# Adjacency masks by casting transfers, x in five loads, powers in pairs, and a search that alone holds the adjacency rooms

## The chip, the cores and the metric

The kernel runs on one core of a Trainium2 chip. Its engines are TensorE (PE; its weight loads, PEld, overlap its matmuls), VectorE (DVE), ScalarE (ACT), GpSimd (POOL) and SyncE (SP, which only issues transfers). ACT and POOL can issue transfers too. Each engine works through its own instructions in order and waits for the others by semaphores. The metric is the time of one execution on the device in microseconds (us), as a median over runs.

## The reference, cut to what matters

x has 2708 rows of 256, adj is 2708 x 2708, float32, about 1.2% of it nonzero, with values up to 1e9. Two layers, each a graph layer and a transformer or expert layer:

```python
# layer 0, graph: adj is added to the logits, so each row's largest entry wins the softmax
x = x + softmax(leaky(f1 + f2.T) + adj) @ h + bias          # h = layernorm(x) @ weight
# layer 0, attention and experts: causal, rotary positions, 4 query and 2 key heads of 64
u = layernorm(x)
z = u + attention(rmsnorm(u)) @ wo.T
x = x + z + top2_of_8_experts(rmsnorm(z))
# layer 1, graph: the mask is adj != 0, or the diagonal
x = x + sigmoid(softmax(where((adj != 0) | eye, leaky(a_src + a_dst.T), -inf)) @ Xp)   # Xp = layernorm(x) @ W.T + b
x = x + top2_of_8_experts(layernorm(x))
```

Because entries of adj are so large, the kernel replaces the first softmax by a lookup: for each row it finds the index of the largest entry and adds that row of h. Flags test whether this holds, and a general network runs if not.

## The kernel before, in words

Rows are cut into NT = 22 tiles of 128 (the last has 20). There are four stages: `first` (0 to about 505 us of the profile), `experts_blocks` of layer 0 (to about 808), `second` (to about 1148), `experts_blocks` of layer 1.

**The planner.** In `first` and `second` every piece of work is a step given to `Plan.add`: an engine, a length in us, a function that emits the instructions, the steps it needs, buffers it takes and gives back, a rank, and `lands`, the time a transfer still takes after its issue. `Plan.issue` simulates the engines with these figures and always emits, among the steps that can start soonest, the one of lowest rank. The figures are used for the order only: what an engine really waits for are semaphores on the data. Before a PE step that the plan sees start late, `fill` emits throwaway matmuls into a free PSUM bank (tile `nobody`), so many that 75% of the gap is filled at 0.24 us each, in gaps of at least 1 us.

**The first stage.** `project` (two tiles at a time, rank -1) takes the statistics of x on DVE (L268, L270, L918), a power -1/2 per tile on POOL (L922), transposes x on PE (L929), multiplies by the centred weight (L949), scales on ACT (L956) and stores the result to the table `hd` in memory (L961). POOL adds the bias row into x (L933). x arrives in three loads of 4, 17 and 1 tiles (L856, L859).

`tile_in` runs once per tile t, with rank t. SP loads 128 rows of adj into one of three rooms in `arena` (L990) together with the rotary table `tb` (L992). DVE finds the eight largest entries (`top`, L995) and the index (`index`, L999). ACT narrows the same room to bfloat16 in two halves (`narrow`, L1009; POOL clears the padding, L1006 and L1008), and SP saves the halves to the matrix `mb` in memory (L1012). A room has two names in the plan, `adj` and `low`: `index` gives back the one and the second narrowing the other, and the next load into it takes both. POOL fetches the chosen rows of `hd` and adds them into x by an indirect transfer (L1017); this needs all stores to `hd`. Then come statistics (DVE), powers (POOL), the q/k/v product (PE), rotary positions on POOL (`both`: L804 to L806 and L1064), transposes, and copies into qT and kT.

`pair` does attention for two tiles of queries, with rank t0 + 2.5: scores on PE (L1121), exponentials on ACT (L1127), the causal mask on POOL (L1136), values on PE (L1147), sums of exponentials on DVE (L1161, L1166; for the first tiles on PE), reciprocal (L1204), the output product, and additions into x. After groups of tiles, `route` chooses two experts per token and POOL scatters the rows to the experts' lists `xs` (`send`, L1830). At the end `early_blocks` runs three expert blocks whose tokens are already complete, after the last scores. The next stage begins with loads of expert rows from `xs`.

**The second stage** reads `mb` by transposing transfers on SP (L1570, L1566), the first of them at 809.8 us, turns it into 0 and 1 on DVE, and sums neighbours on PE (L1603). It has a plan of its own.

Transfers that POOL issues share one queue (q0), those of SP another (q1), those of ACT a third (q10); all run on the same 16 DMA engines. In the cut below, functions that the change touches are shown.

Of the kernel before, what the change touches and what calls it, by code (L numbers as in the profile page):

```python
# [10 lines left out]
F32 = mybir.dt.float32  # L11
# [9 lines left out]
P = 128  # L21
# [53 lines left out]
class Plan:  # L75
# [8 lines left out]
    UNIT = 0.24  # L84
    FILL = 0.75
    GAP_MIN = 1.0
# [64 lines left out]
def adj_ffn_kernel(ctx, tc, x, adj, vecs, bias_rows, tab, w_gnn0, w_gnn1, wqkv, wo,  # L151
# [41 lines left out]

    ident = const.tile([P, P], F32, name="ident")
# [33 lines left out]
    allones = const.tile([P, P], F32, name="allones")  # L228
    nc.gpsimd.memset(allones, 1.0)

# [138 lines left out]

    def route(add, tiles, ready, copied, cleared, layer, XB, xs, pool, turn_tile, turn_bank, gate_tile, gate_bank, rank):  # L370
# [127 lines left out]
        if layer == 0:  # L498
            a = [add("ACT", 0.6, lambda t=t: squares(t), [ready[t - t0]], rank=rank) for t in tiles]
            a = add("DVE", 0.3, mean, a, rank=rank)  # L500
            scaled = add("POOL", 0.9, power, [a], rank=rank)
        last = None
        for pair in pairs:
# [10 lines left out]
            if gate_tile is None:  # L514
                a = add("ACT", 0.25, lambda pair=pair: keep(pair), [a], give=[turn_bank], rank=rank)
            last = a
        a = add("DVE", 3.2, choose, [last], rank=rank)
        b = add("ACT", 0.5, exps, [a], rank=rank)
# [3 lines left out]
        return [add("POOL", 2.7, lambda t=t: send(t), [b, c] + cleared, rank=rank + 6, lands=2.0) for t in tiles]  # L522


    def some_blocks(add, layer, blocks, fetched, needs, weights, xs, acc, new, named, rank):

        joins = []
        for k, (e, j, before) in enumerate(blocks):
# [68 lines left out]
            a = add("ACT", 0.7, back, [a], take=[names["xT"]], give=[names["mm"]], rank=r)  # L597
# [3 lines left out]
            a = add("ACT", 1.4, gate, [a], take=[names["sl"], names["hT"]], rank=r)  # L601
            a = add("DVE", 1.4, times, [a], give=names["up"] + [names["sl"]], rank=r)
# [4 lines left out]
            joins.append(add("POOL", 1.6, join, [a], give=[names["ys"]], rank=r))  # L607
        return joins

    def early_blocks(add, layer, needs, sent, *rest):  # L610
        blocks = [(e, j, (needs if layer == 0 else []) + sum([sent[t] for t in sent if t < before_t], []))
                  for e, j, before_t in EARLY[layer]]

        return some_blocks(add, layer, blocks, [XR[:, k, :] for k in range(len(blocks))], needs, *rest)
# [194 lines left out]
    def first(X, XB, norms, tops, hd, mb, xs, acc, arena, load_weights):  # L809
# [11 lines left out]
        with ExitStack() as s:  # L821
# [24 lines left out]
            def tr_tile():  # L846
                return mm_tile().rearrange("p (k c) -> p k c", c=P)

            plan = Plan(mm=2, mv=4, ix=4, tb=6, st=2, o=1, zs=1, e=4, xg=3, hT=3,
                        z=2, qk=2, es=1, ob=2, yT=2, mb=2, rT=1, adj0=1, adj1=1, adj2=1, low0=1, low1=1, low2=1)  # L850
# [3 lines left out]
            loads = []  # L854
            for a, b in ((0, 4), (4, NT - 1)):
                loads.append(add("SP", 0.5, lambda a=a, b=b: nc.sync.dma_start(  # L856
                    out=X[:, a:b, :], in_=x[a * P:b * P, :].rearrange("(t p) c -> p t c", p=P)),
                    rank=-9.0, lands=1.5 + 0.4 * (b - a)))
            loads.append(add("SP", 0.5, lambda: nc.sync.dma_start(  # L859
                out=X[:rows(NT - 1), NT - 1, :], in_=x[(NT - 1) * P:N, :]), rank=-9.0, lands=9.0))  # L860
            rest = add("ACT", 2.0, load_rest, rank=-9.0, lands=8.0)
# [19 lines left out]
            a = add("SP", 1.2, load_wq, loads, take=["e"], rank=1.5, lands=3.0)  # L881
# [21 lines left out]
            wg_in = add("SP", 0.0, lambda: None, rank=-9.0, lands=3.0)  # L903
# [5 lines left out]
            def project(t0):  # L909
# [5 lines left out]
                def stats(t):  # L915
                    r = rows(t)
                    v["mv", t], v["pv", t] = moments(X[:r, t, :], r), small.tile([P, 1], F32, tag="pv", name="pv")
                    nc.vector.tensor_scalar(v["pv", t][:r], v["mv", t][:r, 1:2], 1.0, 1e-5, ALU.mult, ALU.add)  # L918

                def power(t):  # L920
                    r = rows(t)
                    nc.gpsimd.tensor_tensor(out=rsx[:r, t:t + 1], in0=v["pv", t][:r], in1=mhalf[:r, 0:1], op=ALU.pow)  # L922
# [43 lines left out]

                x_in = [loads[0]] if t0 < 4 else [loads[1]] if t0 + 2 < NT else loads[1:]
                s_ = {t: add("DVE", 0.85, lambda t=t: stats(t), x_in, take=["mv"], rank=rank) for t in two}
                c = [add("POOL", 0.6, lambda t=t: power(t), [s_[t]], give=["mv"], rank=rank) for t in two]
                a = add("PE", 0.5, turn, x_in, take=["mm"], rank=rank - 1.0)  # L970
                for t in two:
                    biased.append(add("POOL", 0.8, lambda t=t: bias(t), [a, s_[t], rest], rank=rank + 1.5 + t / NT))
                a = add("ACT", 0.6, back, [a], take=["yT"], give=["mm"], rank=rank - 1.0)
                a = add("PE", 1.75, times, [a, centred[0]], take=[bank], give=["yT"], rank=rank)
# [4 lines left out]
            made, loaded = {}, {}  # L979
            rsv = ap.tile([P, NT, 2], F32, name="rsv")  # L980
            nmv = ap.tile([P, NT], F32, name="nmv")

            def tile_in(t):
# [4 lines left out]
                def load():  # L988
                    v["a"] = arena[:, t % 3 * N:(t % 3 + 1) * N]
                    nc.sync.dma_start(out=v["a"][:r], in_=adj[t * P:t * P + r, :])  # L990
                    v["tb"] = adjp.tile([P, 2 * HD], F32, tag="tb", name="tb", bufs=6)
# [5 lines left out]
                def index():  # L997
                    v["ix"] = small.tile([P, 8], mybir.dt.uint32, tag="ix", name="ix")
# [1444 lines left out]
```

## Time and profile before

| | us |
|---|---|
| median of three runs (lowest, highest) | 1467.53 (1466.63, 1470.84) |
| the profiled execution | 1465.13 |
| its span from the first to the last instruction | 1463.3 |
| PE, PEld, DVE, ACT, POOL busy | 1385.9, 1006.3, 775.9, 555.3, 525.3 |
| q1, q0 moved | 162.32 MB, 25.71 MB |

Times in views of the trace are us from the span's start unless marked ns. A line of a group gives: line and engine, operation, output and inputs by name, shape, count; then busy time and mean ns of one; then the idle time of the engine just before these instructions and what ended it. A line of waits gives: who waited for what, us in total, times, longest. A line of a stretch gives: the stretch, its length, busy time of each engine with instruction counts, the granted PE clock as a share, the mean busy share of the DMA engines, GB/s. Fillers count as PE busy time.

### The profile page before, as it was taken

How to read it: one execution, taken by the hardware profiler on the slowest of the kernel's cores; microseconds unless marked ns; L12 is line 12 of the kernel's file. 1: busy time of each engine (PE TensorE's matmuls, PEld its weight loads, DVE VectorE, ACT ScalarE, POOL GpSimd, SP SyncE). 2: the span in 40 equal slices, each digit the busy share in tenths (PEclk: the TensorE clock that was granted, in tenths of full speed). 3: DMA queues.
4: the chain of work that ended last, by engine and by line, in shares of the span. 5: the costliest groups of instructions: out<-in, count | busy, mean ns of one | idle time of the engine just before them, and what ended most of it. 6: DMA issues, size and time to landing. Idle time of an engine off the chain costs nothing.

```text
span 1463.3 us, 20902 instructions
## 1 busy us (share of the span) xinstructions
PE 1385.9 (95%) x7218; PEld 1006.3 (69%) x7218; DVE 775.9 (53%) x1680; ACT 555.3 (38%) x1104; POOL 525.3 (36%) x677
## 2 busy tenths in 40 slices
PE   6988989989999999999999899999999999999996
PEld 5643433433343888888788878888768888878885
DVE  5688999985676432222222474768565322322221
ACT  2576867655545322222221444434432211111110
POOL 5576668874224312222222210022334222222222
PEclk9899999999999999999999999999999999999998
DMA  7588756540001277777512770616321687666211
GB/s 268 192 290 287 252 197 226 158 155 31 8 16 64 46 205 185 168 175 197 105 18 26 159 166 1 133 39 151 108 73 58 148 214 187 194 185 129 24 19 21
DMA packets 260056, 193.05 MB, mean 132 GB/s; under 512 B 168008, under 2 KB 232104, under 8 KB 257232
## 3 DMA queue, kind: packets, MB, share of 16 engines
q1 hardware_dynamic: 235638, 162.32, 38.0%
q0 software_dynamic: 20032, 25.71, 9.7%
q10 hardware_dynamic: 4270, 3.58, 0.8%
q8 instruction: 59, 0.97, 0.3%
q14 instruction: 57, 0.47, 0.1%
HBM read 119.81 MB, written 56.11 MB: 120 GB/s over the span
## 4 chain that ended last, share of the span: by engine, by line
PE 77%; DVE 8%; POOL 6%; DMA 5%; issue 2%; ACT 1%; SPq 0%; POOLq 0%; DVEq 0%; ACTq 0%
PE pup L2115 23%; PE po L1603 15%; PE y L2130 13%; PE o L1147 4%; PE stt L1121 4%; PE up L562 3%; DMA X<-hd,ix 3%; PE pup L2146 3%; PE y L2180 1%; DVE yT L1204 1%; DVE es L1166 1%; PE po L949 1%; DVE ix L999 1%; POOL ra L804 1%; DVE tops L995 1%
## 5 line engine op out<-in xcount | busy, mean ns | idle before, releaser
L2115 PE MATMUL pup<-xTs,arena 128*128 128x256 f32 (+2 forms) x1320 | 249.7, 348 | 0.6 <-ACT xTs L2098 0.6
L2115 PEld LDWEIGHTS pup<-xTs,arena 128*128 128x128 f32 (+1 forms) x1320 | 218.5, 189 | 27.2 <-PE y L2180 1.5
L1603 PE MATMUL po<-hb,PT 128*128 128x257 f32 (+2 forms) x968 | 227.6, 389 | 2.9 <-DVE PT L1596 2.9
L2119 ACT ACTIVATE sl<-pup 128x256 f32<-128x256 f32 (+1 forms) x210 | 73.5, 350 | 368.9 <-PE pup L2115 325.4
L1603 PEld LDWEIGHTS po<-hb,PT 128*128 128x128 f32 (+2 forms) x968 | 176.7, 189 | 42.8 <-issue 13.3
L2120 DVE TENSOR_TENSOR hT<-sl,pup 128x256 f32<-128x256 f32 (+1 forms) x210 | 79.6, 380 | 225.8 <-ACT sl L2119 220.5
L1127 ACT ACTIVATE e<-stt 128x1024 f32<-128x1024 f32 (+1 forms) x132 | 125.5, 986 | 93.5 <-PE stt L1121 63.8
L1166 DVE TENSOR_TENSOR es<-es,e 128x1024 f32<-128x1024 f32 x104 | 137.8, 1325 | 29.8 <-ACT e L1127 22.0
L622 POOL DMA_INDIRECT out<-ys,XR x44 | 68.0, 1545 | 234.2 <-DVE ys L2133 149.5
L622 POOL DMA_INDIRECT acc<-ys,XR x44 | 68.3, 1553 | 215.4 <-DVE ys L2133 120.8
L1121 PE MATMUL stt<-qT,kT 64*128 64x512 f32 (+1 forms) x528 | 133.4, 616 | 4.3 <-ACT e L1127 3.9
L2130 PE MATMUL y<-arena,hT 128*128 128x256 f32 x612 | 137.3, 380 | 0.0
L2130 PEld LDWEIGHTS y<-arena,hT 128*128 128x128 f32 x612 | 114.6, 190 | 19.7 <-DVE hid L2154 4.9
L1830 POOL DMA_INDIRECT xs<-XR,place x88 | 93.2, 1059 | 91.8 <-DVE mk L1590 40.2
L1147 PE MATMUL o<-e,V 128*64 128x512 f32 (+1 forms) x528 | 122.4, 586 | 0.0
L1581 ACT ACTIVATE E<-sb,dcol 128x768 f32<-128x768 f32 (+1 forms) x88 | 75.3, 859 | 108.4 <-DVE PT L1596 106.5
L2133 DVE TENSOR_SCALAR ys<-y,XR 128x256 f32<-128x256 f32 x71 | 34.4, 484 | 133.7 <-PE y L2130 133.7
L2115 PE MATMUL pup<-xTs,room 128*128 128x256 f32 (+3 forms) x528 | 99.9, 346 | 0.0
L1121 PEld LDWEIGHTS stt<-qT,kT 64*128 64x128 f32 x528 | 44.7, 188 | 76.5 <-issue 63.0
L2115 PEld LDWEIGHTS pup<-xTs,room 128*128 128x128 f32 (+1 forms) x528 | 85.4, 189 | 9.8 <-PE y L2180 0.8
L1147 PEld LDWEIGHTS o<-e,V 128*64 128x64 f32 x528 | 32.9, 136 | 68.5 <-issue 53.2
L995 DVE MAX8 tops<-arena 128x8 f32<-128x2708 f32 (+1 forms) x22 | 65.3, 2970 | 1.5 <-DMA arena<-in_adj 1.5
(319 smaller groups left out, 1972.1 us busy)
## 6 DMA issues: line engine op xcount, KB each, us to landing
more<-in_w SPq DMA_DIRECT2D x48, 640.0 KB
arena<-in_adj SPq DMA_DIRECT2D x21, 1354.0 KB
arena<-in_w SPq DMA_DIRECT2D x36, 640.0 KB
mb<-mb SPq DMA_DIRECT2D x44, 352.0 KB
xs<-none SPq DMA_DIRECT2D x16, 536.0 KB
room<-in_w SPq DMA_DIRECT2D x12, 640.0 KB
pieces<-xs SPq DMA_DIRECT2D x200, 32.0 KB
acc<-X SPq DMA_DIRECT2D x21, 128.0 KB
```

The source lines that it names most:

```text
L622: i = nc.gpsimd.indirect_dma_start(out=acc[:, :], out_offset=bass.IndirectOffsetOnAxis(ap=tokens.bitcast(I32), axis=0), in_=ys, in_offset= ...
L995: nc.vector.max(out=tops[:r, t, :], in_=v["a"][:r])
L1121: nc.tensor.matmul(st[:r, g, c0(sb):], kT[a:b, sb * P:sb * P + r], qT[a:b, t0 + (sb == t0 + 1):t0 + 2, :, :], start=True, stop=True)
L1127: nc.scalar.activation(e[:r, :, c0(sb):], v[sb, "st"][:r, :, c0(sb):], AF.Exp, scale=1.0 / HD ** 0.5)
L1147: nc.tensor.matmul(v["o"][g * HD:(g + 1) * HD, c:], V[:r, sb, g * HD:(g + 1) * HD], v[sb][:r, g, c:], start=(n + i == 0), stop=(n + i == t ...
L1166: nc.vector.tensor_tensor(es, es, v[sb][:r, :, c:], ALU.add)
L1581: nc.scalar.activation(e[:q, :n], sb[:q, i0:i1], AF.Exp, bias=dcol[:q, j:j + 1], scale=SLOPE - 1.0)
L1603: nc.tensor.matmul(v["po", i][:r, :F], v["PT", j][:q, a:a + r], hb[:q, j, :], start=(j == 0), stop=(j == NT - 1))
L1830: i = nc.gpsimd.indirect_dma_start(out=xs[:, :], out_offset=bass.IndirectOffsetOnAxis(ap=at, axis=0), in_=src, in_offset=None)
L2115: nc.tensor.matmul(pp[:to, i, :B, :], wn[:, c, :], xT[:, c, :B, :], start=(c == 0), stop=(c == KC - 1))
L2120: nc.vector.tensor_tensor(hT[:, n, :B, :], sl[:, :B, :], pp[:, 1, :B, :], ALU.mult)
L2130: nc.tensor.matmul(y, hT[:, n, b, :], w[3][:, n, :], start=(n == 0), stop=(n == NHC - 1))
```

## The change

- **Masks.** `narrow`, `save` and the padding memsets go, and with them the names `low`. After all tiles' steps there are 22 new POOL steps, `cast`: each is one transfer from adj in memory to `mb` in memory that turns float32 into bfloat16. They need the last adjacency load, are chained in the plan one after the other (1.2 us of POOL, 6 us to land), and have ranks from 22 to 32.5. Seven small transfers on SP (`blank`) write the padding of `mb`. The second stage still reads `mb` as before.
- **Search.** The load of a room has rank t - 2 and `tb` a step of its own; `top` and `index` have rank t and not t + 2; only `index` gives the room back. The indices stay in one tile `ixs` and no longer rotate.
- **Start.** x comes in loads of 2, 4, 8, 7 and 1 tiles. `allones` is set first on POOL, and fillers multiply it by itself, not by `before`. Statistics and powers of two tiles share a buffer and one power instruction.
- **Planner.** Many lengths and some `lands` are new; fillers fill 85% of a gap at 0.22 us each, from gaps of 0.7 us. Some needs are added that the order kept by chance so far: routing choices in sequence (`chosen`), additions of expert results after the stores of the same rows (`standing`), last products and joins after the earlier ones. Both stages end in two empty steps behind the scatters, which let `fill` act there. The weights' fold moves from rank 45 to rank 1, the q/k/v product to rank t - 2.5.

```diff
-    UNIT = 0.24
-    FILL = 0.75
-    GAP_MIN = 1.0
+    UNIT = 0.22
+    FILL = 0.85
+    GAP_MIN = 0.7
...
+    allones = const.tile([P, P], F32, name="allones")
+    nc.gpsimd.memset(allones, 1.0)
     ident = const.tile([P, P], F32, name="ident")
...
-            for a, b in ((0, 4), (4, NT - 1)):
-                loads.append(add("SP", 0.5, lambda a=a, b=b: nc.sync.dma_start(
+            loads, ends = [], (2, 6, 14, NT - 1)
+            for a, b in zip((0,) + ends, ends):
+                loads.append(add("SP", 0.55 * (b - a), lambda a=a, b=b: nc.sync.dma_start(
...
+                def power():
+                    for at, q in [((0, 2), P)] if rows(t0 + 1) == P else [((0, 1), P), ((1, 2), rows(t0 + 1))]:
+                        n = at[1] - at[0]
+                        nc.gpsimd.tensor_tensor(out=rsx[:q, t0 + at[0]:t0 + at[1]], in0=v["pv"][:q, at[0]:at[1], 0],
+                                                in1=mhalf[:q, :n], op=ALU.pow)
...
+                def cast():
+                    nc.gpsimd.dma_start(out=mb[t * P:t * P + r, :N], in_=adj[t * P:t * P + r, :])
...
-                a = loaded[t] = add("SP", 5.8, load, take=[f"adj{t % 3}", f"low{t % 3}", "tb"], rank=rank,
-                                    lands=1.5)
-                a = add("DVE", 2.97, top, [a], rank=rank + 2)
-                b = a
-                for h in range(2):
-
-                    b = add("ACT", 1.4, lambda h=h: narrow(h), [b, stored[-1]], take=["mb"], give=[f"low{t % 3}"] * h, rank=rank + 4)
-                    add("SP", 0.4, lambda h=h: save(h), [b], give=["mb"], rank=rank, lands=3.0)
-                a = add("DVE", 3.05, index, [a], take=["ix"], give=[f"adj{t % 3}"], rank=rank + 2)
-                a = add("POOL", 1.6, fetch, [a, biased[t]] + stored, give=["ix"], rank=rank, lands=2.5)
+                a = loaded[t] = add("SP", 3.6, load, take=[f"adj{t % 3}"], rank=rank - 2.0, lands=2.0)
+                tb = add("SP", 0.4, load_tb, take=["tb"], rank=rank, lands=2.2)
+                a = add("DVE", 3.0, top, [a], rank=rank)
+                a = add("DVE", 2.97, index, [a], give=[f"adj{t % 3}"], rank=rank)
+                a = add("POOL", 1.7, fetch, [a, biased[t]] + stored, rank=rank, lands=4.0)
...
+            def blank():
+                zero = none[:, :C].bitcast(BF16)
+                nc.sync.dma_start(out=mb[:, N:].rearrange("(t p) c -> p t c", p=P),
+                                  in_=zero[:, :NT * P - N].unsqueeze(1).to_broadcast([P, NT, NT * P - N]))
+                for a in range(0, N, 2 * C):
+                    b = min(N, a + 2 * C)
+                    nc.sync.dma_start(out=mb[N:, a:b], in_=zero[:NT * P - N, :b - a])
+
+            add("SP", 3.0, blank, [loaded[NT - 1]], rank=NT + 4.0, lands=3.0)
+            last = None
+            for t, cast in enumerate(casts):
+                last = add("POOL", 1.2, cast, [loaded[NT - 1], last], rank=NT + 0.5 * t, lands=6.0)
...
+            a = add("SP", 0.5, lambda: None, sum(sent.values(), []), rank=999.0, lands=4.0)
+            add("PE", 0.5, lambda: None, [a], rank=999.0)
...
-                        nc.tensor.matmul(nobody[:, :P], allones, before, start=True, stop=True)
+                        nc.tensor.matmul(nobody[:, :P], allones, allones, start=True, stop=True)
```

## The prediction

> **What bounds the kernel now.** I read the slices of the page first: 505 us of the span are the first stage, where TensorE's digits stand between 6 and 9; the expert stages stay at 9. All parts of the change but a few planner figures lie in that stage. Then busy time by stretch of it (columns: PE, PEld, DVE, ACT, POOL busy, clock, DMA share, GB/s):
>
> ```profile
> 53.00:150.00 97.00, 82.06 (x376) 41.58 (x376) 79.63 (x78) 69.21 (x125) 69.74 (x100) 0.91 0.86 285
> 150.00:300.00 150.00, 137.52 (x616) 58.59 (x613) 144.90 (x149) 107.59 (x187) 114.08 (x139) 0.99 0.63 206
> 300.00:506.00 206.00, 197.13 (x965) 90.06 (x963) 132.88 (x207) 100.70 (x163) 86.42 (x119) 1.00 0.14 45
> ```
>
> The same stretches for the filler tile `nobody` alone give 16.9, 4.2 and 6.7 us of PE, so its real work is 65, 133 and 190 us: idle 32 of 97, 17 of 150, 16 of 206. DVE is full from 150 to 300 (145 of 150) and had 17 us free before. The end is PE-bound. So time is to be won before 150 us, and it is kept if the DVE-bound stretch moves forward whole. What was awaited there, from the chain in order of time (start, length, what):
>
> ```profile
> 0.82 4.77 DMA X<-in_x
> ...
> 9.29 4.10 PE nobody L1288 x22
> ...
> 19.44 10.29 DMA hd<-hs
> ...
> 57.04 9.35 DMA X<-hd,ix
> 83.15 7.37 DMA X<-hd,ix
> ...
> 112.17 10.10 DMA X<-hd,ix
> ...
> 166.52 8.48 DMA X<-hd,ix
> ...
> 283.30 4.65 DMA X<-hd,ix
> ```
>
> x landed at 5.6, but PE stood until 9.29 for the mask `before` and then ran 22 fillers; the first real matmul came at 13.2. Each chosen row (`fetch`) took 7 to 10 us on busy queues and 4.65 later. The waits of the first stage on DVE and SP agree:
>
> ```profile
> DVE st L268 <- DMA X<-hd,ix: 16.4, 8, 4.1
> ...
> DVE tops L995 <- DMA arena<-in_adj: 1.5, 1, 1.5
> ```
> ```profile
> SPq L1012 <- ACT mb L1009: 134.7, 41, 15.1
> ```
>
> SP stood 134.7 us behind the narrowing, yet the search waited only 1.5 us for adjacency: giving rooms back sooner is worth little by itself. The groups that are removed, and the nearest rows to a POOL-issued transfer:
>
> ```profile
> L1009 ACT CAST mb<-arena 128x1408 bf16<-128x1408 f32 x21 | 28.7, 1366 | 4.6 <-DMA mb<-mb 4.6
> L1009 ACT CAST mb<-arena 128x1300 bf16<-128x1300 f32 x21 | 26.9, 1281 | 0.1
> ...
> L1830 POOL DMA_INDIRECT xs<-XR,place x44 | 48.4, 1099 | 18.3 <-issue 9.3 <-ACT e L1127 7.8 <-DVE XR L479 0.9
> L1017 POOL DMA_INDIRECT X<-hd,ix x22 | 37.2, 1691 | 19.6 <-issue 10.8 <-DVE ix L999 6.8 <-DMA xs<-none 1.9
> ```
>
> [...] No cast is in this trace; POOL's indirect transfers share one queue (q0). [...] 1 KB rows of a fetch took 8 to 10 us beside adjacency loads, 4.65 when the share was lower. [...] Here no row shows memory to memory. [...] POOL's qk sum rises from 1.0 to 1.87 us beside es sums, so POOL has less room than it looks.
>
> **Part by part.**
>
> *Start (allones first, fillers on it, x in five loads).* The first load shrinks from 512 to 256 KB. 512 KB took 4.77; 256 KB takes between 1.5 (a 256 KB store when quiet, 50.45) and 4.77, I take 3.5, so x is there at 4.3. Fillers start at about 1.2 instead of 9.29: 16 by the planner's figures (4.3 x 0.85 / 0.22), at 4.10 / 22 = 0.19 each 3 us, over by then. ACT's queue and table load end at 5.65, so back and times follow at about 7 against 16.6, 9.5 earlier. The two osb buffers then wait for stores of about 10 us beside the first three adjacency loads, as before at 19.44. The 22.2 us from that landing to the last store (29.7 to 51.9) stay: nine pairs of PE 2.5 each. Kept of the 9.5: 4 to 11, I take 8. Powers in pairs: 22 x 0.55 become 11 x about 0.84 (the two-column row), 2.8 us less of POOL, hidden behind PE's pairs: 0.
>
> *Search earlier in rank.* Before, the first search stood at 17.9 in front of the statistics and its index came at 35.6. Now all statistics go first (22 x 0.75 from 4.3, to about 21), then searches of 6 us without a break: four tiles by 45, against three by 53. Some 6 us of search leave the DVE-bound stretch; PE can use perhaps 4.
>
> *No narrowing, no saves.* 42 x 1.33 plus 2.7 for the last tile = 58 us of ACT, 10.7 us of POOL memsets (7.6 + 3.1), 44 saves of 0.36 MB = 15.9 MB beside 29.3 MB of adjacency. ACT was 69% full in the stretch, so its gain alone is 0 (its cover is the PE pace). The traffic falls by a third: a share of 0.86 becomes about 0.6, the share of 150 to 300. A fetch then takes between 4.65 and 8.8 (mean of the four); I take 6: 4 x 2.8 = 11 us, bounds 0 to 16.4 (all that DVE waited).
>
> *Casts on POOL.* 22 transfers of 1.39 MB in, 0.69 out, chained in the plan by 1.2 + 6.0 + 0.2 = 7.4 us after the last adjacency load (issued at 246.0 now; about 200 then, by the 23 us summed below and two tiles of rank, some 11 us each), so to about 363. POOL's share: between 1.0 (scatter of 128 rows)[...]; I take 1.5: 33 us. Free between 200 and 350: 150 - 124 + 6 memsets = 32, and from 350 to 500 105 more. So 0 on the path at 1.5; at 3 us it is 66 and the rope work (4.6 us a tile) behind it on POOL is late, and qT, kT for PE after that. The data: bounds 4.5 us each (adjacency at 308 GB/s) to 14 (half that and slower); I take 7[...] and inside the pace; masks are read at 810. Cover: the 0.1 DMA share from 350 to 500. A fetch or scatter behind one cast waits up to 7 us; the fetches of the last two tiles could, with 15 us of pair work on hand: 0, bound 8. The padding writes (7 on SP, at 0.4 to 0.5 of issue) and the table as a step of its own: 0, SP is free.
>
> *Fillers denser (0.85 / 0.22, gaps from 0.7), planner durations, order edges, empty end steps.* Fillers 28 us become perhaps 33, in gaps: 0 to +2, taken 0. At the end of stage one PE waits from 505 to 509.5 for expert rows anyway: up to 20 fillers of 0.12 are covered. In the second stage PE is busy 328 of 338 us; new figures can win or lose 3, taken 0.
>
> **Sum**: 8 + 11 + 4 = 23. The profiled execution took 1465.1 (span 1463.3); 1465.1 - 23 = 1442. The median of the runs is 2.4 above it: 1444.5. PE's 389 us of real work from the first fetch on would fill 438 us to 89% against 86% now, while the late stretch already runs at 92%: possible.
>
> **Rivals.**
> 1. *Casts clog q0 (slower).* They stand in one queue with the scatters of the last tiles (498.6 to 503.5), and expert rows are fetched at 504.7. From 200 to 475 there is room for 12.5 us a cast, 111 GB/s read. At 14 us the queue ends at 508 and scatters 28 us late, against a stage end of 482: 1444 + 30 = 1474; at 16, about 1510. For: nothing shows the rate, and an issue can stand behind an unrelated transfer (SP's L859 waited 3.5 us for wg, POOL's L1017 1.9 for xs<-none), so a slow cast may hold POOL itself. Against: quiet DMA engines. 12%.
> 2. *POOL becomes the bound.* At 3 us a cast or more, 66 us in 32 of room: up to 34 late, 1444 + 34 = 1478; it ends the gain above 2.5 us. Against: 128 rows cost 1.0 to 1.7 in both rows shown. 8%.
> 3. *Only the start is won.* Fetches stay at 9 us since an adjacency load is still mostly in flight, and DVE fills as before: 1467.5 - 8 = 1459. 14%.
> 4. *Much more is won.* Search so far ahead that PE idles 10 of the 49 us between 53 and 300: 8 + 35 = 43, 1424. 13%.
> 5. *Nothing*: gains meet small losses in the new order, 1467. 5%.
>
> **How the numbers follow.** The forecast has 48%, its own range 1432 to 1456. Within 0.3% (4.4 us, about what a measurement here can tell from no change) is case 5. Faster: forecast, 3 and 4, 75%; same 5%; slower 20%. The low end 1418 leaves out a sliver of case 4, the high end 1476 most of case 1 and half of case 2.
>
> **What would show it.** First real matmul near 4.5, first fetch near 45, last rope before 300, end of stage one near 482. Chain fetches of about 6 us and DVE waiting under 6 us for them. Casts at 1 to 2 us on POOL, q0's share up, DMA share near 0.5 between 200 and 360. Wrong if a scatter or fetch on q0 takes over 15 us, if POOL is over 95% full between 200 and 350, or if the first fetch is no earlier than 50.

## The result, and the profile after

The changed kernel takes 1472.9 us (median of 20 runs, 1464.2 to 1475.9) against 1466.4 for the kernel before: ratio 1.0040, 95% interval 1.0029 to 1.0051. It is slower by 5.9 us where 23 less was forecast. Its profiled execution took 1474.8 us, the span 1472.9.

Most of the difference is there when the first stage ends. A good mark is the reciprocal that closes a pair of tiles (`turn_over`, line 1206 after, 1204 before): the eleventh and last starts at 481.1 us against 476.7, and the first matmul of the expert stage at 516.2 against 508.4. From there to the last of these matmuls both take 933 us. Of the 9.6 us between the two spans, 7.8 are thus there when the expert stage begins; another 2.4 come after the last of these matmuls (23.9 us in place of 21.5), behind the last work that the profile shows, and their cause stays open.

Of the 7.8 us, 4.4 are there at the eleventh reciprocal. The rest comes with fillers that the empty end steps put in front of the first transposes of the expert rows (start, length, what); before has none at that place:

```profile
511.01 4.02 PE nobody L1307 x36
```

The transposes start 5.4 us after the rows are asked for (509.6 to 515.0), before 2.1 (504.7 to 506.9).

Busy time of the changed kernel by stretch, columns as in the prediction:

```profile
53.00:150.00 97.00, 85.44 (x452) 46.46 (x451) 87.69 (x83) 46.04 (x109) 72.28 (x96) 0.96 0.71 217
150.00:300.00 150.00, 136.36 (x570) 55.19 (x572) 137.94 (x152) 81.98 (x165) 113.78 (x131) 0.94 0.58 164
300.00:506.00 206.00, 196.84 (x949) 86.97 (x946) 128.77 (x191) 100.01 (x157) 90.14 (x125) 0.98 0.39 85
```

ACT lost 50 us of work (505 busy in place of 555) and DMA traffic fell from 285 to 217 and from 206 to 164 GB/s, as meant. PE did nothing more with it: without the fillers (20.5, 0.8 and 5.6 us here) its real work is 65, 136 and 191 us, against 65, 133 and 190. DVE was busy 226 of the 247 us from 53 to 300, before 225. And PE ran slower: clock 0.94 from 150 to 300 where it was 0.99.

The chain of waits of the changed kernel (start, length, what), for the start and for the stretch around the first pair:

```profile
1.15 6.28 PE nobody L1307 x32
7.43 0.44 PE pm L941 x4
...
13.91 9.03 DMA hd<-hs
...
33.34 11.47 DMA hd<-hs
...
57.25 3.76 DMA X<-hd,ixs
...
87.46 2.90 DVE tops L1011
...
90.39 3.05 DVE ixs L1014 x2
93.44 2.88 DVE tops L1011
96.32 3.25 DVE yT L1206
...
111.68 8.98 DMA X<-hd,ixs
...
137.64 10.13 DMA X<-hd,ixs
```

The first transposes run at 7.4 in place of 13.2, but two stores of `hd` of 9 and 11 us then stand in the way, and the first fetch is issued at 55.2 (before 53.0). Two later fetches in this chain still take 9 to 10 us. The first reciprocal follows a row of searches on DVE. The waits of the first stage, in us, times, longest:

```profile
ACT hs L968 <- DMA hd<-hs: 16.0, 4, 7.9
...
DVE st L267 <- DMA X<-hd,ixs: 8.2, 6, 3.0
```

ACT's wait for stores was 6.0 us, once, before; DVE's for fetches was 16.4. So that wait halved, and bought nothing. The chain picks out fetches that somebody waited for. For all 22 the times from issue to landing are:

```profile
DMA to landing us min/median/max: 3.8/6.1/10.5
```

The landings in the trace of before give 3.8 to 10.1 us, 6.0 in the median: a typical fetch was not slow before either. The casts, first as POOL has them (durations in ns, first and last start) and then, in the page's list of DMA issues, from issue to landing:

```profile
L1018 POOL DMA_DIRECT2D mb<-in_adj x22: 520/552/1232, 255.7 to 456.4; - x22
```
```profile
mb<-in_adj POOLq DMA_DIRECT2D x21, 677.0 KB, 7.9
```

0.55 us of POOL and 7.9 us for the data: neither of the two slow rivals came true.

### The profile page after: what moved, and what is told of

The parts are those of the page before. It is cut to its first block, busy times and chain, and to the rows that moved or that the text cites. A ratio compares the mean times of both kernels' runs of the same rounds, so it can differ in the third digit from the quotient of the medians.

```text
span 1472.9 us, 20953 instructions
## 1 busy us (share of the span) xinstructions
PE 1401.5 (95%) x7332; PEld 1017.3 (69%) x7332; DVE 780.4 (53%) x1670; ACT 505.4 (34%) x1060; POOL 529.2 (36%) x666
## 3 DMA queue, kind: packets, MB, share of 16 engines
q0 software_dynamic: 23104, 40.38, 15.0%
## 4 chain that ended last, share of the span: by engine, by line
PE 76%; DVE 10%; POOL 6%; DMA 4%; issue 2%; ACT 1%; POOLq 0%; DVEq 0%; ACTq 0%
PE pup L2144 23%; PE po L1622 15%; PE y L2159 13%; PE o L1149 4%; PE stt L1123 4%; PE up L565 3%; PE pup L2175 3%; DVE ixs L1014 2%; DVE tops L1011 2%; DMA X<-hd,ixs 2%; DVE yT L1206 2%; PE y L2209 1%; DVE es L1168 1%; DMA hd<-hs 1%; PE nobody L1307 1%
## 5 line engine op out<-in xcount | busy, mean ns | idle before, releaser
L1149 PE MATMUL o<-e,V 128*64 128x512 f32 (+1 forms) x528 | 127.5, 606 | 0.0
L1014 DVE FIND_INDEX8 ixs<-tops,arena 128x8 uint32<-128x2708 f32 (+1 forms) x22 | 65.4, 2972 | 0.0
```

What stands on the lines that cost most here:

```text
L1014: nc.vector.max_index(out=ixs[:r, t, :], in_max=tops[:r, t, :], in_values=v["a"][:r])
L1149: nc.tensor.matmul(v["o"][g * HD:(g + 1) * HD, c:], V[:r, sb, g * HD:(g + 1) * HD], v[sb][:r, g, c:], start=(n + i == 0), stop=(n + i == t ...
```

## The experiments

Each ran in five rounds beside the kernel before, whose median was 1466.3 to 1469.6 us from one group of experiments to the next; so ratios against it, with the 95% interval, are what compares, and not the medians. "Searches" counts how many tiles' searches (maximum and index, 6 us a tile) stand in DVE's order ahead of the reciprocals of pairs 1 to 6; the reciprocals are those of the profiled execution, in us.

| kernel | median us | ratio | searches ahead of pairs 1 to 6 | reciprocal of pair 1, 4, 7, 10, 11 |
|---|---|---|---|---|
| before | 1466.4 | 1 | 6 9 12 15 17 20 | 94 179 294 429 477 |
| changed | 1472.9 | 1.0040 | 8 10 14 16 19 21 | 96 178 298 433 481 |
| e4 start alone | 1469.7 | 1.0025 (1.0015–1.0034) | 6 9 12 14 17 19 | 90 182 297 432 480 |
| e1 changed, loads held | 1472.6 | 1.0034 (1.0024–1.0043) | as changed | 95 176 294 429 477 |
| e10 before, no narrowing | 1470.8 | 1.0007 (0.9991–1.0023) | as before | 90 178 293 428 476 |
| e11 changed, no casts | 1479.0 | 1.0061 (1.0041–1.0082) | as changed | 96 178 295 429 477 |
| e9 before, casts alone | 1497.9 | 1.0205 (1.0186–1.0224) | 7 11 15 17 20 22 | 95 195 328 460 508 |
| e13 e9, search earlier | 1497.2 | 1.0187 (1.0168–1.0206) | 7 11 15 17 20 22 | 92 193 327 459 507 |
| e12 e9, projections earlier | 1469.4 | 1.0003 (0.9992–1.0014) | 7 11 13 15 18 20 | 93 179 301 430 477 |
| e3 changed, old figures | 1461.7 | 0.9968 (0.9955–0.9980) | 7 10 13 15 17 19 | 89 167 293 421 472 |
| e7 e3, loads held | 1464.3 | 0.9973 (0.9962–0.9984) | as e3 | 90 168 294 422 472 |
| e5 changed, old durations | 1467.8 | 0.9992 (0.9976–1.0007) | as e3 | 89 167 293 421 470 |
| e6 changed, old fillers | 1474.6 | 1.0046 (1.0029–1.0063) | as changed | 97 178 295 430 477 |
| e2 changed, old search ranks | 1475.4 | 1.0056 (1.0038–1.0073) | as changed | 98 181 299 434 482 |
| e14 changed, one figure | 1475.5 | 1.0048 (1.0034–1.0062) | as changed | 97 178 296 430 478 |
| e15 changed, one figure | 1475.5 | 1.0050 (1.0031–1.0068) | 8 10 14 15 19 21 | 98 178 301 427 478 |
| e16 e3, one figure | 1464.1 | 0.9972 (0.9960–0.9983) | as e3 | 89 167 290 419 467 |
| e17 e3, end steps | 1466.1 | 0.9982 (0.9970–0.9993) | as e3 | 88 165 292 421 470 |
| e18 changed, search edges | 1475.2 | 1.0059 (1.0038–1.0080) | 7 9 12 15 17 19 | 89 170 288 420 478 |
| e19 e3, tight edges | 1494.3 | 1.0189 (1.0175–1.0203) | 6 8 10 12 14 16 | 87 166 284 437 497 |

Three theories stood at the beginning. A: rooms given back early let adjacency loads collide with the stores at the start. B: the search, ranked earlier, stands in order ahead of the pairs and makes gaps on PE. C: the planner's new figures (lengths of steps, fillers, added needs, end steps) give a worse order.

### The start

Start alone, on the kernel before (the five loads, the paired powers and the fillers' operand as in the change):

```diff
+    allones = const.tile([P, P], F32, name="allones")   # now ahead of ident
-            for a, b in ((0, 4), (4, NT - 1)):
+            loads, ends = [], (2, 6, 14, NT - 1)
+            for a, b in zip((0,) + ends, ends):
```

> The kernel before with the start alone (the all-ones matrix first and the fillers on it, x in five loads, powers in pairs); masks are narrowed and saved as before. My sum gives 8 us less, 1458, with the first fetch near 45. Theory A says the same, since here a room is given back only after its narrowing and no further adjacency load travels beside the stores: first fetch at 47 or earlier, 5 to 8 us less. If the stores at the start are slow whatever travels beside them, or the gain is lost later, the first fetch stays at 52 to 53, or comes earlier with the time within 2 us of the kernel before.

The first fetch came at 47 and the first reciprocal at 89.9, 4.4 us ahead of before; by the fourth pair it was 3 behind (182), and by its ratio the kernel was 3.6 us slower. So the start did what it says, and the next 90 us took it back. Which wait took it is not settled; the mean clock of its runs was 0.979 against 0.983.

In the changed kernel the start is not even visible at the first fetch. To test why, the fourth to sixth adjacency loads were put on ACT's queue behind its last store of `hd`:

```diff
-                    nc.sync.dma_start(out=v["a"][:r], in_=adj[t * P:t * P + r, :])
+                    (nc.scalar if 3 <= t < 6 else nc.sync).dma_start(out=v["a"][:r], in_=...)
```

> The changed kernel, with the fourth, fifth and sixth adjacency loads issued by ACT behind its last store of hd, so that they can't travel beside the stores. Theory A (the start's gain was lost because rooms given back early let these loads go out at 32 to 46 us, where they slow the hd stores that the first fetch waits for): the long stores of the chain (9.0 and 11.5 us) fall to 6 or less, the first fetch comes at 50 or earlier in place of 55.2, and the time falls by 3 to 6 us against the changed kernel, to 1467 to 1470. Theory B (the loss comes later: DVE's search stands in order ahead of the pairs, PE stands for 3 to 5 us at several places, and each such gap costs a stretch at half clock): the first fetch may move, the gaps between 90 and 340 us stay, the time stays within 2 us of the changed kernel.

Theory B's half clock as the trace of the changed kernel has it: PE's gaps of 3.1 to 5.2 us begin at 96.8, 146.9, 222.7, 250.3 and 327.8 us, and the granted clock was 0.50 from 99 to 105, 150 to 156, 225 to 231, 256 to 258.5 and 331 to 337 us, in each gap or up to 2 us behind it. Between these stretches (106 to 149, 157 to 224, 232 to 255, 260 to 330) it was 1.00.

The chain of waits of the kernel with held loads:

```profile
13.28 9.55 DMA hd<-hs
...
48.12 13.38 DMA X<-hd,ixs
```

The 11.5 us store left the chain and the first fetch went out at 46, as theory A says. But the held loads, issued at 46 and 47, now met the fetches: the one in the chain took 13.4 us, and its rows were there at 61.5. The first such rows in the chain of the changed kernel are there at 61.0, of the start alone at 61.6 (51.5 + 10.0), before at 66.4 (57.04 + 9.35). So some 5 us of the start do reach the first fetched rows in all three, whether stores or fetches pay for the loads; theory A names a real collision (three fetches took 11 to 13 us beside the held loads, 4 in the changed kernel), and it is not what costs the time. With the better order of e3 the same edit changed nothing either:

> The kernel with all planner figures of before (start, casts, early rooms and search ranks as changed: 1461.7), with the fourth to sixth adjacency loads behind the last store of hd as in the earlier run with such loads. If the earlier first fetch is worth something once the order is better: first fetch at 46 to 48 in place of 53 and 3 to 6 us less, 1456 to 1459. If the pace after the first fetch is set by what PE and DVE have to do, as the earlier run suggests: first fetch at 46 to 48 and the same time, 1460 to 1464.

First fetch at 49 in place of 53, ratio 0.9973 against 0.9968.

### The narrowing that was removed, and the casts

The term "no narrowing, no saves" was run by itself, in the planned order of the kernel before. All tiles but the first are neither narrowed nor saved, and the second stage reads the first tile's mask throughout.

```diff
                 def narrow(h):
+                    if t:
+                        return
                 def save(h):
+                    if t:
+                        return
```

> The kernel before in its own planned order, but the narrowing and the saving of all tiles but the first are left out (the second stage reads the first tile's mask for every tile, so the output is not the reference's): what the removed work was worth by itself, without any new order. My sum gave 11 us (bounds 0 to 16.4) for shorter fetches: 1456, chain's fetches near 6 us. Rival theory (order decides, the pairs' pace doesn't feel the fetches): 0 to 3 us less, 1464 to 1467.

No change within the interval, whose lower end (0.9991) leaves room for a gain of 1.3 us. As the second stage works on other masks here, the first stage is the cleaner mark, and it agrees: the first matmul of the expert stage comes at 507.8, before 508.4. Its stretches, fetches from its chain of waits, and DVE's wait for fetches:

```profile
53.00:150.00 97.00, 84.22 (x384) 42.61 (x384) 81.20 (x80) 46.90 (x107) 70.18 (x93) 0.90 0.72 232
150.00:300.00 150.00, 140.34 (x605) 60.50 (x605) 140.37 (x149) 81.01 (x161) 104.80 (x124) 0.95 0.47 143
```
```profile
56.80 9.39 DMA X<-hd,ix
...
103.68 9.04 DMA X<-hd,ix
...
138.82 10.31 DMA X<-hd,ix
...
164.62 9.35 DMA X<-hd,ix
```
```profile
DVE st L268 <- DMA X<-hd,ix: 17.7, 13, 3.5
```

The DMA share fell from 0.86 to 0.72 and from 0.63 to 0.47. The four fetches above took 9 to 10 us; all eight of the chain from 53 to 300 us took 4.6 to 10.3, 7.9 in the mean, where the five of before took 4.7 to 10.1, 8.0 in the mean; and DVE waited 17.7 us for them, before 16.4. That is the forecast's largest term refuted at its own place: this fall of the share did not shorten a fetch. Adjacency loads of 1.35 MB remain and are issued in the same stretch; that a slow fetch waits for those is the likely reason (it fits e1, where fetches beside three of them took 11 to 13 us), and no run took them away.

The casts' cost in the changed order, by leaving 21 of the 22 out:

```diff
                 def cast():
+                    if t:
+                        return
```

> The changed kernel in its own planned order, but 21 of the 22 casting transfers are left out (the second stage reads the first tile's mask for every tile, so the output is not the reference's). My sum costs the casts at 0: within 2 us of the changed kernel, 1471 to 1475. If they cost through POOL's order or through the scatters queued behind them: 4 to 8 us less, 1465 to 1469, with PE's gaps at 250 and 328 us gone.

Nothing comes back: 1.0061, where the changed kernel itself has 1.0040, with intervals that overlap (1.0041 to 1.0082, 1.0029 to 1.0051). The first stage of the profiled execution does end 3.6 us earlier than in the changed kernel (512.6 against 516.2), but so it does in e14 and e15 (512.8 each), which keep all casts. The gaps of PE at 248 and 325 us stay too, so they are not the casts' doing. In this order the casts cost nothing that these runs can tell, as forecast.

### Casts without the other ranks

Casts alone on the kernel before (narrowing, saves and their rooms replaced as in the change, everything else old):

```diff
-                a = loaded[t] = add("SP", 5.8, load, take=[f"adj{t % 3}", f"low{t % 3}", "tb"], rank=rank,
+                a = loaded[t] = add("SP", 5.4, load, take=[f"adj{t % 3}"], rank=rank, lands=1.5)
-                    b = add("ACT", 1.4, lambda h=h: narrow(h), ...)
+                casts.append(cast)
```

> The kernel before with the casting transfers alone: no narrowing, no saves, rooms given back by the search; start, ranks, durations and fillers as before. My sum gave 11 us for the traffic that goes: 1455, with the chain's fetches at about 6 us in place of 8.8. Rival (a late fetch is covered once pairs are on hand, so that PE's work sets the pace): fetches shorter but the time within 4 us of the kernel before, 1463 to 1467. If casts in POOL's order delay the rope work: slower, 1470 or above.

30 us slower. Its chain of waits from 100 to 200 us:

```profile
103.25 6.36 DMA X<-hd,ixs
...
112.61 7.24 DMA X<-hd,ixs
...
145.75 9.79 DMA X<-hd,ixs
...
162.78 8.27 DMA X<-hd,ixs
```

Here the chain runs from fetch to fetch, with statistics, searches and a pair's work between: fetches are 38% of it. PE's real work from 150 to 300 fell to 114 us (129.1 less 14.8 of fillers). The first cast starts at 218 and can't explain reciprocals that are late from the second pair on (124 us, before 115; 195 against 179 at the fourth). Removing the narrowing had also changed the plan: rooms (`low`) had been given back only after it, at four ranks behind the load. That this had paced loads and search is the likely reason, and the count agrees (15, 17, 20 and 22 searches ahead of pairs 3 to 6, before 12, 15, 17 and 20); no run kept the old pace with the casts in. Two runs ask which other part of the change makes up for it.

```diff
e13:
-    load, ..., rank=rank        top, [a], rank=rank + 2        index, ..., rank=rank + 2
+    load, ..., rank=rank - 2.0  top, [a], rank=rank            index, ..., rank=rank
e12:
-    times, [a, centred[1]], ..., rank=rank        weight_folds(add, af, mm_tile, [rest], 45.0)
+    times, [a, centred[1]], ..., rank=rank - 2.5  weight_folds(add, af, mm_tile, [rest], 1.0)
```

> The kernel before with casting transfers, and the search and its loads two tiles earlier in rank (projections and folds stay). If the search, no longer held back by the narrowing's rooms, had to be ranked earlier to keep the fetches ahead of the pairs: most of the 30 us come back, 1462 to 1472. If the projections' ranks did it: 1490 or above.

> The kernel before with casting transfers alone took 1497.9, 30 us more than before, though start, search ranks and all else together with them took 1461.7. This adds to it the ranks of the projection's matmuls (2.5 tiles earlier) and of the weight folds (first instead of at 45). If PE's projections came too late behind pairs, and so POOL's rope: most of the 30 us come back, 1462 to 1472. If not: 1490 or above, and the search's ranks or the start did it.

The search's ranks give back nothing clear of the intervals. The ranks of projections and folds, moved together, give back the 30 us whole. The prediction did not price that edit at all.

### The planner's figures

Theory B put the loss on the new search ranks:

> The changed kernel with the ranks of the adjacency loads and of the search as in the kernel before (load at the tile's rank, search two tiles later). Theory B: PE's gaps over 3 us between 90 and 340 us (96.8, 146.9, 222.7, 250.3, 327.8) mostly go, the clock time lost in the first stage falls from 20.5 to about 14 us, and the time falls by about 5 us, to 1468. Theory A: first fetch still near 55, time within 2 us of the changed kernel. If the search was a gain after all, this is 2 to 4 us slower than the changed kernel.

The edit is e13's in reverse, on the changed kernel. The count of searches ahead stayed 8 10 14 16 19 21, and the time did not fall: these ranks are not what put the searches there, so theory B has the wrong cause.

Then all planner figures of before, keeping start, casts, rooms and ranks (`UNIT`, `FILL`, `GAP_MIN`, every duration, no order edges, no end steps):

```diff
-    UNIT = 0.22
-    FILL = 0.85
+    UNIT = 0.24
+    FILL = 0.75
-    a = add("POOL", 1.7, fetch, ..., lands=4.0)      a = add("POOL", 4.0, both, ...)
+    a = add("POOL", 1.6, fetch, ..., lands=2.5)      a = add("POOL", 3.4, both, ...)
```

> The changed kernel with all planner durations, filler constants and order edges of the kernel before and without the empty end steps; start, casts, early rooms and search ranks stay. Theory C (the loss is one of order: new durations put instructions in a worse order, and the end step adds fillers ahead of the expert rows, 3.5 us at the end of the stage): the wait and fillers from 505 us on fall back by 3 to 4 us and the time falls by 4 to 8 us, to 1465 to 1469. Theories A and B: the long stores and PE's gaps stay, time within 2 us of the changed kernel, at best 3.5 less through the tail.

1461.7 us: faster than both kernels, by 0.32% against before and by 0.72 points (10.6 us) against the changed one, with intervals far apart. The same work runs here; only the order and the fillers differ. This is theory C, except that the gain is larger than it said. The new figures are, where the trace shows the thing, the truer ones: a fetch lands after 6.1 us in the median (4.0 in place of 2.5 in the plan), the rotary work ("rope") on POOL takes 4.4 a tile (four rows of 0.97 to 1.27; 4.0 in place of 3.4). With them the plan puts up to two more searches ahead of the first six reciprocals (the table); presumably it takes the pairs to be ready later.

The figures were then split. Durations back, fillers, edges and end steps new:

> The changed kernel with the planner's durations of the kernel before; the denser fillers, the order edges and the empty end steps stay as changed. With durations, fillers, edges and end steps all put back together the kernel took 1461.7. Theory F1 (the new durations put DVE's and POOL's instructions in a worse order between 90 and 180 us): this takes 1462 to 1465, with the third pair's reciprocal near 141 and the fifth's near 167 as there. Theory F2 (the fillers, edges and end steps are what costs): 1470 to 1474, with 3 to 4 us of fillers standing ahead of the expert rows at the end of the stage.

Fillers and end steps back, durations and edges new:

> The changed kernel with only the filler constants of before and without the empty end steps; new durations and edges stay. Theory F2: 1462 to 1466. Theory F1: only the 3.5 us at the end of the stage come back, 1469 to 1471, and the gaps of 3 us and more between 90 and 340 us stay; [...] 1472 or above.

End steps alone added to e3:

> The kernel with all planner figures of before (1461.7), with the empty end steps of both stages added. They change no order of other work, and add fillers at the stages' ends. If the fillers of the end stand ahead of the expert rows: 2 to 4 us more, 1464 to 1466. If PE waits for the rows there anyway: within 1 us, 1461 to 1463.

Durations give back 7 us of the 10.6 (1.0040 to 0.9992); the remaining 3.5 show only once the durations are back, since old fillers with new durations give nothing (1.0046), though there the transposes of the expert rows do start 2.1 us after their request again. End steps account for perhaps 2 of it (0.9982 against 0.9968; the intervals overlap). Is it one figure, or a draw among orders?

```diff
e14:  -  add("POOL", 1.05, sum_up    +  add("POOL", 1.1, sum_up       (e16: the reverse, on e3)
e15:  -  add("ACT", 0.94, exps       +  add("ACT", 1.0, exps
```

> The changed kernel with one planner figure put back, that of the sum into x on POOL (1.1 for 1.05), which no instruction's own work depends on. Theory G (the planner's order turns over with any figure, so the 11 us between old and new figures are a draw among orders): the time moves by 3 us or more either way from 1473. Theory H (the new figures as a set are worse, each by a little): within 2 us of 1473.

> The changed kernel with one planner figure put back, that of the exponentials on ACT (1.0 for 0.94). Theory G: the time moves by 3 us or more either way from 1473, or, if not, the other single figures do. Theory H: within 2 us of 1473.

> The kernel with all planner figures of before (1461.7), with one figure changed to the new one, that of the sum into x on POOL (1.05 for 1.1). Theory G: 3 us or more from 1462, more likely upward, since 1462 would be a good draw. Theory H: within 2 us of 1462.

By the ratios each moved the time by 0.6 to 1.5 us, within the intervals. All eight kernels with the new durations lie between 1.0034 and 1.0061, and the five with the change's ranks and the old durations between 0.9968 and 0.9992 (e19, whose edges are a change of their own, left out). So the set matters. These three single figures speak against a draw among orders; others were not tried.

### The search's place by itself

All new figures kept; only the plan's search is held behind the reciprocals:

```diff
-                a = add("DVE", 3.0, top, [a], rank=rank)
+                a = topped[t] = add("DVE", 3.0, top, [a], rank=rank)
...
                 a = add("DVE", 3.4, turn_over, [a], ...)
+                for n in (7, 10, 13, 15, 17, 19)[t0 // 2:t0 // 2 + 1]:
+                    for u in range(n, NT):
+                        topped[u]["needs"].append(a)
```

> The changed kernel with planner edges alone: the search of the tiles from the 8th, 11th, 14th, 16th, 18th and 20th on is planned after the reciprocal of the first, second, third, fourth, fifth and sixth pair. In the changed kernel 8, 10, 14, 16, 19 and 21 searches stand ahead of these reciprocals in DVE's order; in the kernel with the old planner figures (1461.7) 7, 10, 13, 15, 17 and 19; here 7, 9, 12, 15, 17 and 19. Theory S (the new figures cost by putting searches of 6 us ahead of the pairs' reciprocals in DVE's order): 1463 to 1468, first reciprocal near 90, third near 141, fifth near 210. If the 11 us lie elsewhere: 1471 to 1475.

The reciprocals came as theory S says: 89, 136 and 209 for pairs 1, 3 and 5, in the changed kernel 96, 149 and 222; at pair 10 they were still 13 us ahead (420 against 433). The time was the changed kernel's all the same. Its chain at the end of the stage, and its stretches there:

```profile
452.96 1.26 POOL xs L1862
...
457.11 2.77 DMA xs<-XR,place
...
460.97 11.14 DMA XR<-xs
```
```profile
464.00:472.00 8.00, 0.97 (x4) 0.29 (x2) 0.00 (x0) 1.21 (x3) 0.00 (x0) 0.72 0.98 218
472.00:480.00 8.00, 7.90 (x40) 6.18 (x41) 1.95 (x1) 1.91 (x3) 0.00 (x0) 0.64 0.01 2
```

At the same place e3 has:

```profile
460.53 5.35 DMA XR<-xs
```

The casts of e18 come later: seven were issued between 371 and 387, five at 444 to 460 and the last at 489 (in e3 the last four at 445 to 459). The rows of the first expert block, asked for at 461 behind three casts issued from 458 on, took 11.1 us; in e3, behind two, 5.4. PE stood for 7 of 8 us with the DMA engines 98% full, and then ran at a clock of 0.64. Most of the lead went there: the eleventh reciprocal is only 3 us ahead (478 against 481). If the casts did it, that is rival 1 of the prediction in miniature: not the scatters behind the casts in q0 but the fetch after them, and only where the casts reach the end of the stage. But one cast more than in e3 is little to go by, and moving them away in this order was not tried. So that the search's place costs the time is shown up to the tenth pair and not for the whole kernel.

> The kernel with all planner figures of before (1461.7), with such edges drawn tighter: 6, 8, 10, 12, 14, 16, 18 and 20 searches ahead of the first eight reciprocals, so that DVE's 132 us of search spread over more pairs. Theory S: the stretch from 53 to 300 us, where DVE is over 90% full, gets room: 1455 to 1460. If a lead of four tiles is too short for the fetches and the rope work behind them: 1466 or above, with PE waiting for qk.

One to three searches fewer again were too few: the last fetch went out at 370 (changed: 284) and the reciprocals of pairs 10 and 11 at 437 and 497. Here a lead of four tiles does not feed the pairs.

## Why the prediction was wrong

Two steps failed above all. The largest gain, shorter fetches, was worth 0, and the planner's figures, put at 0, cost 10.6 us. In the order of the sum:

- **Start, 8 us.** Half right at the first rows, gone at the end. x landed at 4.4 (4.3 forecast), but PE's first transposes came at 7.4, not 4.5: the plan set 32 fillers of 6.3 us (16 of 3 us forecast). The first fetched rows of the chain were there 5 us earlier, not 8. Alone (e4) the start was 4.4 us ahead at the first reciprocal, and the kernel 3.6 us slower. The step that the 22.2 us from the first landing to the last store would stay missed that stores meet more adjacency loads once rooms are given back early: ACT waited 16.0 us for stores in place of 6.0, and from that landing (22.9) to the first fetch (55.2) it took 32 us, before 23. (The 1.5 us taken as a lower bound is a store of 20 rows, not of 256 KB; in the trace of before, stores of 256 KB issued from 30.7 to 48.6 us landed after 2.1 to 2.3 us, at a DMA share of 0.28 from 30 to 50. The sum doesn't rest on it.)
- **Search earlier, 4 us.** Not seen. The ranks alone won 2 to 3 us, within the intervals (e13 against e9, the changed kernel against e2). Searches did leave the DVE-bound stretch, 14 tiles searched by 150 us in place of 12, but PE's real work from 53 to 150 stayed at 65 us: "PE can use perhaps 4" is what failed. The sum counted searches that leave, and not that each stands ahead of a reciprocal that PE waits for. In the changed kernel it is the durations that put more of them there: pairs 3 to 10 closed 5 to 15 us later than in e3 (178 against 167 at pair 4), and the edges of e18 won that back up to pair 10.
- **No narrowing, no saves, 11 us.** Nothing (e10). The step that failed is the fall of a fetch from 8.8 to 6 us with the traffic. The share fell to 0.72, not 0.6, and the 8.8 was the mean of the four longest fetches in the chain; all 22 took 6.0 us in the median before, and still 6.1 in the changed kernel. DVE's wait for them stayed at 17.7 us in e10. It did halve in the changed kernel (8.2), but also in e3 (7.9), which is 10.6 us faster, so it is not what sets the time.
- **Casts on POOL, 0.** Right in this order (e11): 0.55 us of POOL (1.5 taken), 7.9 us of data (7 taken). Both were the author's estimates: the trace of before has no transfer from memory to memory. The bound of 8 and rival 1 further took it that a scatter or fetch waits for the cast ahead of it in q0. The casts did go through q0 (40.38 MB there in place of 25.71), but no run shows such a wait: the 44 scatters of the first stage landed after 2.1 to 6.6 us, 2.6 in the median. The casts ran from 256 to 456 us and not from 200 to 363, since the last adjacency load was issued at 222.5 (200 forecast) and the first cast stood still later in POOL's order. Its cover was named as the quiet time from 350 to 500; e18 shows what may be lost when they run into the rows' fetch.
- **Fillers, durations, edges, end steps, 0.** The largest miss: 10.6 us by e3, 7 of them by the durations (e5). The prediction priced durations as if only fillers followed from them; the order of DVE's and POOL's work follows too. Of the fillers that the end steps bring it held up to 20 for covered by PE's wait for the expert rows; the plan set 36 (4.0 us). The ranks of `times` and of the folds, not priced, are worth 30 us once the narrowing is gone from the plan (e9, e12).

With the ratios of before at 1466.5 us the change adds up as: casts alone +30; projections' ranks −30; start, search ranks and the new operand of the fillers together −5; new figures +11; in all +6. The parts depend on each other: the start alone cost 3.6 us in the old order, and here it is part of a gain.

Rival 5, "gains meet small losses in the new order", comes nearest, with the gains too large and the loss too small. "Only the start is won" held the right remark, that fetches stay as they are, and the wrong remainder. The measured time lies where rivals 1 and 2 were put (1474 and 1478), but neither happened, so that is chance. (Rival 4's sum is 4 short: 10 of 49 us leaves 39, not 35.) The condition set for "wrong", a first fetch no earlier than 50, was met (55.2); POOL was not over 95% full (114 of 150 from 150 to 300) and no fetch or scatter took over 15 us (10.5 and 6.6 the longest). The last rope was to come before 300 and came at 346.

Two things stay open. One is why a lead of 10 us and more at pair 4 shrinks: e3 is 11 ahead of before there and 1 at pair 7, then 5 at the end. The other is the share of the clock: the runs of the changed kernel had a mean clock of 0.9785 against 0.983, and among its own runs the time falls by about 1.1 us for each 0.001, so some 5 us of the 6 go along with it. But e5 has a higher clock than e3 (0.984 against 0.982) and is slower, so it is not the one cause.

## What to carry over

In a kernel whose order a planner writes, price an edit in two runs: the work taken away in the old order (here 0), and the new order with the old work. Before pricing, count in the order itself how many instructions stand ahead of the one that the bound engine waits for. Don't take the length of a transfer from the pieces of the chain alone: they are there because they were late (8.8 us, where the median of all was 6.0). A change of planner durations is a change of order, also where each new figure is nearer the truth, and a wait that is taken away (rooms held for the narrowing) may have paced the plan.

## What was not expected of the hardware

A casting transfer of 128 rows from memory to memory cost POOL 0.55 us in the median and 0.64 in the mean; the mean of a scatter of 128 rows was 1.08 us (88 in the page) and of a fetch 1.74. 1.39 MB read and 0.69 MB written landed in 7.9 us in the median.

Fetches of 128 rows of 1 KB took 3.8 to 10.1 us, 6.0 in the median, in the kernel before (DMA share 0.86 from 53 to 150 us), 3.8 to 10.5, 6.1 in the median, in the changed kernel (0.71 there), and 11.1 to 13.4 us right beside three adjacency loads (e1). Two stores of `hd` of 9.0 and 11.5 us stand in the chain of the changed kernel, where the DMA share was 1.02 from 14 to 25 us and 0.86 from 33 to 45; with the fourth to sixth adjacency loads held back (e1) the second of them is gone from the chain, and ACT waited 8.4 us for stores in place of 16.0.

In the changed kernel the stretches around PE's four gaps of 3.1 to 5.2 us that begin between 96 and 251 us ran at clocks of 0.74 to 0.86:

```profile
90.00:105.00 15.00, 9.90 (x41) 4.20 (x37) 14.69 (x14) 5.80 (x10) 9.77 (x15) 0.78 0.65 193
145.00:158.00 13.00, 7.79 (x29) 3.69 (x28) 10.86 (x11) 4.86 (x8) 7.20 (x11) 0.74 0.68 236
220.00:235.00 15.00, 11.88 (x41) 4.31 (x37) 11.53 (x6) 4.34 (x10) 9.68 (x15) 0.77 0.77 210
250.00:262.00 12.00, 8.51 (x33) 2.97 (x33) 11.18 (x12) 5.96 (x11) 11.14 (x14) 0.86 0.60 124
```

That is 1.7 to 3.5 us of clock in each (an estimate from these lines: length times what the clock lacks to 1, so 12 us at 0.86 and 15 us at 0.77), part of which falls into the gap itself; in each lies one of the stretches at 0.50 named under e1. Single gaps are not all of it: before had a clock of 0.83 from 120 to 140 us, and 0.52 from 128 to 135, without a gap of 3 us (the longest of PE from 97 to 135 us was 2.3). What brings the lower clock these runs do not show.
